# Four-layer sparse graph network: eager projection steps, whole first-layer rows, output by blocks

## The chip, the cores and the metric

The kernel runs on one core of one Trainium2 chip. The metric is the device time of the launch in microseconds, the median of several runs; lower is better. The engines named below are PE (matrix products and transposes), DVE (vector work), ACT (scalar engine), POOL (here it issues the indirect transfers) and SP (it issues the plain transfers).

## The reference

Sixteen graphs share one adjacency matrix of 1024 nodes, of which a fraction 0.0078 of the entries is set; each node of each graph has a row of 128 numbers. Four layers follow one another. Layers 0, 2 and 3 are attention blocks with 8 heads of 16, masked by the adjacency; layer 1 is a graph attention with one head.

```python
# layers 0, 2, 3
Q, K, V = h @ Wq, h @ Wk, h @ Wv                      # 8 heads of 16
scores = where(adj == 0, -inf, Q K^T / 4)             # per head
x = layer_norm(h + (softmax(scores) V) @ Wo + bo)
x = layer_norm(x + relu(x @ W1 + b1) @ W2 + b2)
# layer 1
h = x @ W;  e = leaky_relu(h a_src [i] + h a_dst [j]);  e = where(adj == 0, -inf, e)
x = layer_norm(softmax(e) h + x)
```

## The kernel before

The kernel works on the lists of neighbours and not on the full matrix. A setup of some 100 us reads the adjacency, sorts the nodes by degree and makes lists of neighbours. After it a tile `t` (8 of them) holds 128 nodes of similar degree, and `places` holds their row numbers in the input and the output. The graphs are split into two groups of 8 (`GR`), and each group again into two halves of 4 (`HF`, the index `h`).

A unit, or block, is one layer, one group and one tile; there are 4 x 2 x 8 = 64, numbered from 0 in that order, so that 0 to 7 are layer 0 with the first group, 8 to 15 layer 0 with the second, 48 to 63 the last layer. For a block the kernel gathers, by an indirect transfer on POOL (line 942), the keys and values of up to two neighbours of each node at a time, multiplies them with the queries on DVE (954), adds up the heads (977), takes exponentials on ACT (981), multiplies with the values on DVE (1005) and sums over the neighbours on PE with 0/1 matrices (1021). One such round is a piece; a block has 4 to 6 of them. At the end of a block `divided` divides by the sums (1058, 1061), and `attention_tail`, one generator for each half, does the rest of the layer (output projection, norms, feed-forward) while the next block's pieces run. Its last step is `finish`: in layers 0 to 2 it projects the result into the next layer's table of keys and values in DRAM, and in the last layer it transposes back into a tile `outs` and sends it by an indirect transfer on POOL to the rows of `out` (676), one transfer of 256 KB for each half.

Everything is issued in an order written out by hand: `manual_schedule`, with generators that are advanced a step at a time. Each engine executes its own instructions in that order. The main loop (line 1152) goes over the pieces and calls `others` three times for a piece of an attention layer. `others` advances the tails at a pace, and then one step of the first thing it finds among `fronts` (the next block's queries, slot lists and weights), `loads` (the input of the block after the next) and `slow`. `slow` is `at_leisure(1)` (772): the projection of the second group's rows into the keys and values of layer 0, 16 half-tiles of three steps each (transposes; two graphs' projection; the other two graphs', after which the table is written). It is advanced only while no tail is in its last stage, or while it is itself in the middle of a half-tile:

```python
def idle():
    return slow if held[0] or not busy[0] else []
```

The first group's rows are projected in the setup (`at_once`). Gathers run four pieces ahead. The first gather of block 8 needs the second group's whole table, so `gathered` (929) first drains what is left of `slow`.

`loaded` (840) fetches the input of a block. In layer 0 that is, for each half, an indirect transfer on POOL of 256 KB into a buffer `rows`, and, some steps later, four transposes on PE and a copy on ACT into the input buffer `x`. `x` has four buffers. The buffer of the second half has the tag of the query buffer `q`.

Of the kernel before, what the change touches and what calls it, by code (L numbers as in the profile page):

```python
# [14 lines left out]
F32 = mybir.dt.float32  # L15
# [7 lines left out]
P = 128  # L23
D = 128
# [113 lines left out]
def sparse_path(ctx: ExitStack, tc: tile.TileContext, a: dict, out: bass.AP, flag):  # L138
# [42 lines left out]
    idx = const.tile([P, 2, T, J, QUADS], I32, name="idx")  # L181
    marks = const.tile([P, len(MARK), 32], F32, name="marks")
    nc.gpsimd.memset(marks, 0.0)
    places = const.tile([P, GR, HF, T], I32, name="places")
    bad = const.tile([P, T], F32, name="bad")
    seen = const.tile([P, 2, G * H], F32, name="seen")
    nc.gpsimd.memset(seen, 0.0)
# [38 lines left out]
    def graph(wide):  # L226
# [148 lines left out]
                q = row_of(t, j)  # L375
                nc.vector.tensor_copy(there[rows, t : t + 1], node[rows, q : q + 1])
        for g in range(GR):
            for h in range(HF):
                nc.vector.tensor_scalar(
                    places[:, g, h, :], there, float(GR * HF), float(g * HF + h),  # L380
                    ALU.mult, ALU.add,
                )
        low = s1.tile([P, T], F32, name="low")
        nc.vector.tensor_tensor(bad, sorted_[:, :, 2], caps[:, :T], ALU.is_gt)
        nc.vector.tensor_scalar(low, sorted_[:, :, 2], 1.0, None, ALU.is_lt)
# [252 lines left out]
    def turned(z, dst, gain=None, shift=None, dve=False):  # L638

        ps = bank([P, GH, P])  # L640
        for i in range(GH):
            nc.tensor.transpose(ps[:, i, :], z[:, i, :], ident)  # L642
        if dve and gain is None:
            nc.vector.tensor_copy(dst, ps)
        elif dve:
            nc.vector.tensor_scalar(dst, ps, gain, shift, ALU.mult, ALU.add)
        elif gain is None:
            nc.scalar.copy(dst, ps)  # L648
        else:
            nc.scalar.activation(dst, ps, AF.Identity, bias=shift, scale=gain)  # L650

    def over_graphs(v):
        return v.rearrange("p (o d) -> p o d", o=1).to_broadcast([P, GH, D])

    def finish(l, g, t, h, z, gain, shift, dve=False):
        if l + 1 < len(LAYERS):

            wanted[0] = True
            while held[0]:
                advance(slow)  # L660
            wanted[0] = False
            busy[0] += 1
            xn = states.tile([P, GH, P], F32, tag="xT", name="xT")
            turned(z, xn, gain, shift)
            yield "free"
            yield from project(l + 1, g, t, h, xn)
            busy[0] -= 1
            return
        xn = states.tile([P, GH, P], F32, tag="xT", name="xT")
        turned(z, xn, gain, shift, dve)  # L670
        yield
        o = twos.tile([P, GH, D], F32, tag="kv", name="outs")
        turned(xn, o, dve=dve)
        yield
        yield
        nc.gpsimd.indirect_dma_start(  # L676
            out=out.rearrange("n (k c) -> (n k) c", k=GR * HF),
            out_offset=bass.IndirectOffsetOnAxis(ap=places[:, g, h, t : t + 1], axis=0),
            in_=o.rearrange("p g d -> p (g d)"), in_offset=None,
        )  # L680

    def hidden():
        return ones_.tile([P, F * GH * P], F32, tag="f1", name="f1")
# [74 lines left out]
    def natural(g, t, h, rows, kv=None):  # L758

        xn = states.tile([P, GH, P], F32, tag="xT", name="xT")  # L760
        turned(rows, xn)
        yield
        yield from project(0, g, t, h, xn, kv)
# [7 lines left out]

    def at_leisure(g):
        def fetch(k):
            rows = ones_.tile([P, GH, D], F32, tag="xg", name="xg")
            if k < T * HF:
                nc.sync.dma_start(
                    rows.rearrange("p g d -> p (g d)"),
                    a["x"][k // HF * P : (k // HF + 1) * P, columns(g, k % HF)],
                )
            return rows  # L780

        rows = fetch(0)
        yield
        for k in range(T * HF):
            steps = natural(g, k // HF, k % HF, rows)
            held[0] = True
            next(steps)
            rows = fetch(k + 1)
            yield
            yield from steps  # L790
            held[0] = False
            if wanted[0]:
                yield
# [46 lines left out]
    def loaded(u):  # L840

        if u >= len(units):
            return
        l, g, t = units[u]
        xs[units[u]] = inputs.tile([P, HF, GH, P], F32, tag="x", name="x")
        if l == 0:
            def fetch(h):
                if u == 0:
                    rows = twos.tile([P, GH, D], F32, tag="o", name="rows")
                else:  # L850
                    rows = ones_.tile([P, GH, D], F32, tag="q" if h else "rows", name="rows")
                nc.gpsimd.indirect_dma_start(
                    out=rows.rearrange("p g d -> p (g d)"), out_offset=None,
                    in_=a["x"].rearrange("n (k c) -> (n k) c", k=GR * HF),
                    in_offset=bass.IndirectOffsetOnAxis(ap=places[:, g, h, t : t + 1], axis=0),
                )
                return rows

            rows = fetch(0)
            yield "idle"  # L860
            yield "idle"
            yield
            turned(rows, xs[units[u]][:, 0])
            rows = fetch(1)
            yield "idle"
            yield "idle"
            yield
            turned(rows, xs[units[u]][:, 1])
            yield
            return  # L870
        nc.sync.dma_start(
            xs[units[u]].rearrange("p h g n -> p (h g n)"),
            kept[l, g][t].rearrange("p h c -> p (h c)"),
        )
# [220 lines left out]
    def others():  # L1095
        pace[0] += pace[1]
        while pace[0] >= 1.0:
            advance(tails)
            pace[0] -= 1.0
        while True:  # L1100
            gens = fronts or loads or idle()
            if not gens:
                break
            got = next(gens[0], "end")
            if got == "end":
                gens.pop(0)
                continue
            if got == "idle":
                advance(idle())
            break  # L1110

    with tc.manual_schedule():
        wide = [gather_buffer() for _ in range(EDGES)]
# [38 lines left out]
        for i in range(len(parts) + 2):  # L1152
            here = i < len(parts)
            u = parts[i][0] if here else len(units)
            if here:
                l = units[u][0]
                if i and parts[i - 1][0] != u:
                    begun = i
                    if u < T - 1:
                        fronts.append(islice(rest, 4))  # L1160
                    if l + 1 < len(LAYERS) and LAYERS[l + 1][1] is ATTN:
                        if units[u][1:] == (0, 1):
                            more = load_weights(LAYERS[l + 1][0])
                            next(more)
                            next(more)
                        if units[u][1:] == (0, 4):
                            fronts.append(more)
                if is_attention(u):
                    products(i)
            if i > 1:  # L1170
                summed(i - 2)
                done = parts[i - 2][0]
                if parts[i - 1 : i] == [] or parts[i - 1][0] != done:
                    closing = divided(done)
                    next(closing)
            others()
            if here:
                exponentials(i)
            if here and i == begun + 1:
                if is_attention(u):  # L1180
                    shared(u)
                while loads:
                    advance(loads)
                if u + 1 < len(units):
                    fronts.append(queries(u + 1))
                loads.append(loaded(u + 2))
                if u:
                    advance(loads)
            others()
            if 0 < i <= len(parts):  # L1190
                weighted(i - 1, 0)
                if not is_attention(parts[i - 1][0]):
                    others()
                    weighted(i - 1, 2)
                gathered(i - 1 + AHEAD)
                for _ in sizes:
                    pass
            if closing is not None and here:
                while any(gen not in free for gen in tails):
                    advance(tails)  # L1200
                next(closing)
                sizes, closing = closing, None
                passes = 3 if is_attention(u) else 4
                steps = STEPS if is_attention(done) else GRAPH_STEPS
                steps -= LATE[units[done][0]]
                pace[:] = 0.0, steps / (passes * sum(part[0] == u for part in parts) - 1)
            others()
            if i + 1 >= len(parts) or parts[i + 1][0] != u:

                while fronts:  # L1210
                    advance(fronts)
# [441 lines left out]
```

## Time and profile before

| | us |
|---|---|
| median of three runs | 2280.79 |
| lowest and highest | 2275.02, 2287.53 |
| span of the profiled execution | 2290.8 |
| PE, DVE, ACT, POOL busy in it | 2052.0, 1871.1, 1530.3, 1050.7 |

The page gives no time of the profiled execution beside its span. Times in the timelines are counted from the start of the span. The end of a block, where it is needed, is taken at the reciprocal on DVE (line 1058). Busy time of an engine says how full it is over the whole span; what a stage waits for is read from the timelines and waits of that stage. Blocks 2 to 6 take 40.6 to 42.1 us each, block 7 takes 46.0, block 8 takes 44.5, blocks 9 to 14 take 36.5 to 37.7, layer 1's blocks 12 to 25, and those of the last layer 36.3 to 41.4, but for the last, 28.4.

### The profile page before, as it was taken

The page shows a single profiled execution, that of the slowest core. Times are in us where ns is not written, and L with a number is a line of the kernel's source. Part 1 is how long each engine was busy: PE and PEld are TensorE (multiplying, and loading weights), DVE is VectorE, ACT ScalarE, POOL GpSimd, SP SyncE. Part 2 cuts the span into 40 slices and gives each one's busy share as a digit, 9 for nine tenths or more (in the row PEclk, how much of TensorE's full clock was granted, in tenths as well). Part 3 has the DMA queues.
Part 4 walks back from the last instruction along what each step waited for, and adds up shares of the span by engine and source line. Part 5 has one row for each costly group of instructions (what it writes and reads, how often), then busy time and mean ns, then how long its engine had stood idle before and what let it go on. Part 6 is the DMA issues. An engine that isn't in the chain of part 4 may idle for free. (4 is left out here: it accounts for less than half of the span.)

```text
span 2290.8 us, 36572 instructions
## 1 busy us (share of the span) xinstructions
PE 2052.0 (90%) x13140; PEld 1271.6 (56%) x13140; DVE 1871.1 (82%) x1472; ACT 1530.3 (67%) x5041; POOL 1050.7 (46%) x730
## 2 busy tenths in 40 slices
PE   6479999899998999998899989999999988998987
PEld 5336666555555555554465655655655555555544
DVE  7898888588888477777988889988888887988783
ACT  3237777777776565556677777777777766776765
POOL 3355344245445278884443434333344444444540
PEclk8789999999999999999999999999999998999999
DMA  7868888678887699997998978888887877677750
GB/s 249 278 217 300 304 279 305 240 247 302 285 295 265 197 330 354 354 373 288 326 318 292 319 254 306 296 314 295 281 282 277 291 258 250 242 275 270 260 217 20
DMA packets 165197, 636.06 MB, mean 278 GB/s; under 512 B 35064, under 2 KB 37880, under 8 KB 116510
## 3 DMA queue, kind: packets, MB, share of 16 engines
q0 software_dynamic: 89216, 485.08, 59.3%
q1 hardware_dynamic: 75792, 148.57, 18.9%
q8 instruction: 105, 1.72, 0.3%
q14 instruction: 84, 0.69, 0.1%
HBM read 581.08 MB, written 92.34 MB: 294 GB/s over the span
## 5 line engine op out<-in xcount | busy, mean ns | idle before, releaser
L942 POOL DMA_INDIRECT e<-table,idx x576 | 844.2, 1466 | 1022.1 <-DVE pr L1005 796.6
L1005 DVE TENSOR_TENSOR pr<-e,ex 128x2048 f32<-128x2048 f32 (+1 forms) x320 | 661.3, 2075 | 55.9 <-ACT ex L981 32.7
L954 DVE TENSOR_TENSOR pr<-e,qr 128x2048 f32<-128x2048 f32 x192 | 439.7, 2290 | 160.3 <-DMA e<-table,idx 91.5
L1021 PE MATMUL acc<-pr,marks 128*32 128x512 f32 x2624 | 528.5, 616 | 20.3 <-DVE pr L1005 16.4
L977 DVE TENSOR_REDUCE sc<-pr 128x128 f32<-128x2048 f32 (+1 forms) x240 | 497.5, 2073 | 8.0
L620 ACT ACTIVATE z<-yps,root 128x128 f32<-128x128 f32 x888 | 319.0, 390 | 35.6 <-PE yps L735 16.8
L1021 PEld LDWEIGHTS acc<-pr,marks 128*32 128x32 f32 x2624 | 108.7, 111 | 280.9 <-issue 231.6
L635 ACT ACTIVATE z<-yps,rstd 128x128 f32<-128x128 f32 x888 | 255.0, 371 | 7.2
L731 PE MATMUL yps<-W,f 128*128 128x128 f32 x1520 | 252.6, 283 | 7.7 <-ACT f L726 1.9
L726 ACT ACTIVATE f<-ps,b 128x512 f32<-128x512 f32 x190 | 130.6, 695 | 160.4 <-PE ps L717 159.7
L731 PEld LDWEIGHTS yps<-W,f 128*128 128x128 f32 x1520 | 205.7, 193 | 51.7 <-issue 26.2
L572 PE MATMUL ps<-Wkv,xT 128*128 128x256 f32 x768 | 212.2, 417 | 20.0 <-ACT xT L648 14.4
L908 ACT COPY qr<-ps 128x512 f32<-128x512 f32 x384 | 197.1, 602 | 47.7 <-PE ps L905 47.7
L642 PE MATMUL ps<-ident,z 128*128 128x128 f32 x896 | 179.7, 300 | 41.4 <-ACT z L635 36.6
L642 PEld LDWEIGHTS ps<-ident,z 128*128 128x128 f32 x896 | 116.2, 143 | 167.7 <-ACT z L635 86.5
L717 PE MATMUL ps<-x,W 128*128 128x512 f32 x384 | 193.9, 630 | 12.5 <-ACT x L650 12.4
L620 ACT ACTIVATION_READ_ACCUMULATOR z<-yps,root 128x1 f32 x888 | 203.7, 229 | 0.0
L905 PE MATMUL ps<-q,rep 32*128 32x512 f32 x768 | 166.5, 661 | 36.4 <-ACT q L900 34.0
L572 PEld LDWEIGHTS ps<-Wkv,xT 128*128 128x128 f32 x768 | 146.5, 204 | 73.9 <-ACT qr L908 18.0
L981 ACT ACTIVATE ex<-sc 128x128 f32<-128x128 f32 (+1 forms) x240 | 76.4, 318 | 157.9 <-DVE sc L977 157.8
L576 ACT COPY kv<-ps 128x512 f32<-128x512 f32 x176 | 103.3, 593 | 108.1 <-PE ps L572 85.8
L706 PE MATMUL yps<-Wo,oT 128*128 128x128 f32 x768 | 159.9, 291 | 10.0 <-ACT oT L648 10.0
(174 smaller groups left out, 2724.2 us busy)
## 6 DMA issues: line engine op xcount, KB each, us to landing
table<-kv SPq DMA_DIRECT2D x88, 512.0 KB
kept<-xT SPq DMA_DIRECT2D x96, 256.0 KB
x<-kept SPq DMA_DIRECT2D x48, 512.0 KB
qx<-qr SPq DMA_DIRECT2D x48, 256.0 KB
e<-table,idx POOLq DMA_INDIRECT x576
table<-kv SPq DMA_DIRECT2D x32, 256.0 KB
qx<-qr SPq DMA_DIRECT2D x18, 384.0 KB
qx<-qr SPq DMA_DIRECT2D x42, 128.0 KB
```

Of the source, the lines that this page charges most:

```text
L572: nc.tensor.matmul(ps[:, k, :], x[:, i + k, :], w[LAYERS[l][0], "Wkv"], start=True, stop=True,)
L620: nc.scalar.activation(z[:, i, :], y[:, i, :], AF.Square, scale=D**-0.5, bias=root, accum_out=total[:, i : i + 1],)
L635: nc.scalar.activation(z[:, i, :], y[:, i, :], AF.Copy, scale=rstd[:, i : i + 1])
L642: nc.tensor.transpose(ps[:, i, :], z[:, i, :], ident)
L717: nc.tensor.matmul(ps, p["W1"][:, f * P : (f + 1) * P], x1.rearrange("p g n -> p (g n)"), start=True, stop=True,)
L731: nc.tensor.matmul(ps[:, i, :], f1[:, f, i * P : (i + 1) * P], p["W2"][:, f, :], start=(f == 0), stop=False,)
L908: nc.scalar.copy(qs[u][:, j, h * GH * D : (h + 1) * GH * D], pss[j])
L942: nc.gpsimd.indirect_dma_start(out=es[i][:, k, :], out_offset=None, in_=tables[l, g][:, :], in_offset=bass.IndirectOffsetOnAxis(ap=idx[:, ...
L954: nc.vector.tensor_tensor(prs[i][0][:, :n, :], es[i][:, :n, :ROW], qx[u].rearrange("p (o c) -> p o c", o=1) if (MIX, 0) in piece else of_p ...
L977: nc.vector.tensor_reduce(sc[:, :n, :], prs[i][0][:, :n, :].rearrange("p k (a d) -> p k a d", d=HD), mybir.AxisListType.X, ALU.add,)
L1005: nc.vector.tensor_tensor(prs[i][k0 // 2][:, :m, :].rearrange("p k (a d) -> p k a d", d=d), es[i][:, k0 : k0 + m, base : base + ROW].rearr ...
L1021: nc.tensor.matmul(outs[32 * j : 32 * j + 32], marks[:, mark, :], rhss, start=(chunk == mine[0]), stop=(chunk == mine[-1]),)
```

## The change

- `places` holds one row number for each node and group, and no longer one for each half; `halves` holds those of the very last block, for each half.
- Output: both halves of a block are written into one tile `outs` of 512 KB, and one indirect transfer sends it when the second half is done. The very last block keeps a transfer for each half.
- The rows of the second group in `at_leisure` have two buffers, `xg` and `xh`, and are fetched two half-tiles ahead.
- `loaded` fetches a block's layer-0 rows with one indirect transfer of 512 KB straight into the input buffer `x`; each half is transposed on PE and copied back by ACT into the same place.
- `others` ends with one more step of `idle()`, that is of `slow`, while the current block is 0 or 1.

```diff
     def finish(l, g, t, h, z, gain, shift, dve=False):
...
-        o = twos.tile([P, GH, D], F32, tag="kv", name="outs")
-        turned(xn, o, dve=dve)
-        yield
-        yield
-        nc.gpsimd.indirect_dma_start(
-            out=out.rearrange("n (k c) -> (n k) c", k=GR * HF),
-            out_offset=bass.IndirectOffsetOnAxis(ap=places[:, g, h, t : t + 1], axis=0),
-            in_=o.rearrange("p g d -> p (g d)"), in_offset=None,
-        )
+        if h == 0:
+            leaving[g, t] = twos.tile([P, HF, GH, D], F32, tag="kv", name="outs")
+        o = leaving[g, t]
+        turned(xn, o[:, h], dve=dve)
+        yield
+        yield
+        if (l, g, t) == units[-1]:
+            nc.gpsimd.indirect_dma_start(
+                out=out.rearrange("n (k c) -> (n k) c", k=GR * HF),
+                out_offset=bass.IndirectOffsetOnAxis(ap=halves[:, h : h + 1], axis=0),
+                in_=o[:, h].rearrange("p g d -> p (g d)"), in_offset=None,
+            )
+        elif h + 1 == HF:
+            nc.gpsimd.indirect_dma_start(
+                out=out.rearrange("n (k c) -> (n k) c", k=GR),
+                out_offset=bass.IndirectOffsetOnAxis(ap=places[:, g, t : t + 1], axis=0),
+                in_=o.rearrange("p h g d -> p (h g d)"), in_offset=None,
+            )
...
     def at_leisure(g):
         def fetch(k):
-            rows = ones_.tile([P, GH, D], F32, tag="xg", name="xg")
+            rows = ones_.tile([P, GH, D], F32, tag=("xg", "xh")[k % 2], name="xg")
...
-        rows = fetch(0)
+        ahead = [fetch(0), fetch(1)]
         yield
         for k in range(T * HF):
-            steps = natural(g, k // HF, k % HF, rows)
+            steps = natural(g, k // HF, k % HF, ahead.pop(0))
             held[0] = True
             next(steps)
-            rows = fetch(k + 1)
+            ahead.append(fetch(k + 2))
...
     def loaded(u):
...
-            def fetch(h):
-                if u == 0:
-                    rows = twos.tile([P, GH, D], F32, tag="o", name="rows")
-                else:
-                    rows = ones_.tile([P, GH, D], F32, tag="q" if h else "rows", name="rows")
-                nc.gpsimd.indirect_dma_start(
-                    out=rows.rearrange("p g d -> p (g d)"), out_offset=None,
-                    in_=a["x"].rearrange("n (k c) -> (n k) c", k=GR * HF),
-                    in_offset=bass.IndirectOffsetOnAxis(ap=places[:, g, h, t : t + 1], axis=0),
-                )
-                return rows
-
-            rows = fetch(0)
-            yield "idle"
-            yield "idle"
-            yield
-            turned(rows, xs[units[u]][:, 0])
-            rows = fetch(1)
-            yield "idle"
-            yield "idle"
-            yield
-            turned(rows, xs[units[u]][:, 1])
+            x = xs[units[u]]
+            nc.gpsimd.indirect_dma_start(
+                out=x.rearrange("p h g d -> p (h g d)"), out_offset=None,
+                in_=a["x"].rearrange("n (k c) -> (n k) c", k=GR),
+                in_offset=bass.IndirectOffsetOnAxis(ap=places[:, g, t : t + 1], axis=0),
+            )
+            for h in range(HF):
+                yield "idle"
+                yield "idle"
+                yield
+                turned(x[:, h], x[:, h])
             yield
             return
...
             if got == "idle":
                 advance(idle())
             break
+        for _ in range(eager[0]):
+            advance(idle())
+
+    eager = [1]
...
                 l = units[u][0]
+                eager[0] = 1 if u < 2 else 0
```

More of the change, by code (lines that the diff above doesn't have):

```diff
@@ L183, in sparse_path @@
     nc.gpsimd.memset(marks, 0.0)
-    places = const.tile([P, GR, HF, T], I32, name="places")
+    places = const.tile([P, GR, T], I32, name="places")
+    halves = const.tile([P, HF], I32, name="halves")
     bad = const.tile([P, T], F32, name="bad")
@@ L377, in graph @@
         for g in range(GR):
[L378 to L381, printed above, removed]
-                )
+            nc.vector.tensor_scalar(
+                places[:, g, :], there, float(GR), float(g), ALU.mult, ALU.add,
+            )
+        for h in range(HF):
+            nc.vector.tensor_scalar(
+                halves[:, h : h + 1], there[:, T - 1 :], float(GR * HF), float((GR - 1) * HF + h),
+                ALU.mult, ALU.add,
+            )
         low = s1.tile([P, T], F32, name="low")
@@ L653, in over_graphs @@
         return v.rearrange("p (o d) -> p o d", o=1).to_broadcast([P, GH, D])
+    leaving = {}
     def finish(l, g, t, h, z, gain, shift, dve=False):
@@ L671, in finish @@
         yield
-        o = twos.tile([P, GH, D], F32, tag="kv", name="outs")
-        turned(xn, o, dve=dve)
+        if h == 0:
+            leaving[g, t] = twos.tile([P, HF, GH, D], F32, tag="kv", name="outs")
+        o = leaving[g, t]
+        turned(xn, o[:, h], dve=dve)
         yield
         yield
-        nc.gpsimd.indirect_dma_start(
-            out=out.rearrange("n (k c) -> (n k) c", k=GR * HF),
-            out_offset=bass.IndirectOffsetOnAxis(ap=places[:, g, h, t : t + 1], axis=0),
-            in_=o.rearrange("p g d -> p (g d)"), in_offset=None,
-        )
+        if (l, g, t) == units[-1]:
[9 more added lines that the diff above has]
+                in_=o.rearrange("p h g d -> p (h g d)"), in_offset=None,
+            )
     def hidden():
@@ L846, in loaded @@
         if l == 0:
-            def fetch(h):
-                if u == 0:
-                    rows = twos.tile([P, GH, D], F32, tag="o", name="rows")
-                else:
-                    rows = ones_.tile([P, GH, D], F32, tag="q" if h else "rows", name="rows")
-                nc.gpsimd.indirect_dma_start(
-                    out=rows.rearrange("p g d -> p (g d)"), out_offset=None,
-                    in_=a["x"].rearrange("n (k c) -> (n k) c", k=GR * HF),
-                    in_offset=bass.IndirectOffsetOnAxis(ap=places[:, g, h, t : t + 1], axis=0),
-                )
-                return rows
-            rows = fetch(0)
-            yield "idle"
-            yield "idle"
-            yield
-            turned(rows, xs[units[u]][:, 0])
-            rows = fetch(1)
-            yield "idle"
-            yield "idle"
-            yield
-            turned(rows, xs[units[u]][:, 1])
+            x = xs[units[u]]
[3 more added lines that the diff above has]
+                in_offset=bass.IndirectOffsetOnAxis(ap=places[:, g, t : t + 1], axis=0),
+            )
+            for h in range(HF):
+                yield "idle"
+                yield "idle"
+                yield
+                turned(x[:, h], x[:, h])
             yield
```

## The prediction

> **What bounds the kernel now.** I read the page first, then the stage table by blocks (a block is one unit: layer, group, tile; its end is the reciprocal of line 1058), then the waits of each engine, and at the two stalls the timelines.
>
> The first part of the page:
>
> ```profile
> PE 2052.0 (90%) x13140; PEld 1271.6 (56%) x13140; DVE 1871.1 (82%) x1472; ACT 1530.3 (67%) x5041; POOL 1050.7 (46%) x730
> ```
>
> PE and DVE share the load, so each stage has to be asked. The stage table (length, PE, PEld, DVE, ACT, POOL, clock, DMA share, GB/s): blocks 0 and 1; block 4; block 7; block 10; a layer-2 block; a last-layer block.
>
> ```profile
> 101.00:162.50 61.50, 34.17 (x151) 14.06 (x151) 57.66 (x77) 10.98 (x25) 29.34 (x17) 0.72 0.68 249
> 162.50:203.20 40.70, 37.80 (x252) 24.79 (x252) 35.81 (x39) 30.63 (x99) 17.80 (x12) 1.00 0.77 274
> 328.50:370.00 41.50, 38.74 (x258) 25.63 (x258) 35.51 (x38) 31.07 (x102) 18.15 (x12) 1.00 0.83 291
> 410.60:456.70 46.10, 39.94 (x246) 27.22 (x247) 25.78 (x16) 30.79 (x98) 15.65 (x12) 0.93 0.64 229
> 575.30:612.70 37.40, 34.72 (x237) 22.10 (x235) 32.21 (x18) 28.21 (x98) 18.31 (x12) 1.00 0.85 296
> 1438.10:1474.70 36.60, 34.39 (x229) 21.66 (x229) 32.24 (x20) 27.60 (x88) 14.18 (x10) 1.00 0.91 321
> 2110.50:2148.50 38.00, 33.17 (x216) 20.02 (x216) 32.12 (x20) 27.04 (x87) 18.10 (x12) 1.00 0.72 264
> ```
>
> Block 0 leaves PE idle for 27 us. Blocks 2 to 6 take some 41.5 us and blocks 9 to 14 some 37: the former also carry the second group's projection (two half-tiles each). Block 7 is the longest, though it has the fewest pieces. The last layer has less PE work than layer 2 and is slower.
>
> Block 7 on SP, POOL and DVE (start, length):
>
> ```profile
> 416.72 0.57 SPq L581 DMA_DIRECT2D table<-kv  x1
> 422.34 4.04 SPq L581 DMA_DIRECT2D table<-kv  x2
> 429.70 0.99 POOL L942 DMA_INDIRECT e<-table,idx  x1 [27.85 <-DMA table<-kv]
> 432.00 2.29 DVE L1005 TENSOR_TENSOR pr<-e,ex 128x2048 f32<-128x2048 f32 x1 [10.37 <-ACT ex L981]
> ```
>
> The drain of line 930 emits the last three half-tiles at once; the first gather of the second group waits 27.85 us for their tables, and the exponential that DVE needs stands behind their copies on ACT.
>
> A last-layer block, on ACT, POOL and DVE:
>
> ```profile
> 2072.84 0.59 ACT L648 COPY outs<-ps 128x512 f32<-128x512 f32 x1 [0.27 <-PE ps L642]
> 2075.65 2.11 POOL L676 DMA_INDIRECT out<-outs,places  x1 [0.30 <-ACT qr L908]
> 2084.50 2.32 POOL L676 DMA_INDIRECT out<-outs,places  x1 [6.74 <-ACT rstd L627]
> 2087.12 1.95 POOL L942 DMA_INDIRECT e<-table,idx  x1 [0.31 <-ACT z L620]
> 2097.07 2.29 DVE L954 TENSOR_TENSOR pr<-e,qr 128x2048 f32<-128x2048 f32 x1 [5.46 <-DMA e<-table,idx]
> ```
>
> And DVE's waits from 1696 to 2224 us (total, times, longest):
>
> ```profile
> DVE pr L954 <- DMA e<-table,idx: 62.8, 14, 5.9
> ```
>
> The second half's data are ready at 2073.4, yet its output goes at 2084.50, and the gathers behind it on POOL go later still. The releaser printed had nothing to do with it. What did, the chain that ended last shows, at the very end where nothing else runs:
>
> ```profile
> 2282.70 0.99 DMA out<-outs,places
> 2283.69 2.30 issue
> ```
>
> Output h=1 follows output h=0 only when that has landed: both write the tensor `out` at rows taken from a table, so the second is ordered behind the first. In the stream that costs POOL some 6 us of waiting and DVE 4.5 us (62.8 / 14) in each of blocks 49 to 62.
>
> **The Trainium skill.** "DMA: Bandwidth & Descriptors", section "Anatomy of one DMA — SWDGE (gpsimd) path": a semaphore wait is made on the issuing sequencer before dispatch, so it holds what is behind; the trace agrees (2075.65 to 2087.12 without a gather). It prices a DMA at 2.0 us plus bytes / 436e3: an estimate of 2.6 us for 256 KB; the trace has 3.5 us (2282.70 to 2286.19) alone and 8.4 to 8.9 among gathers, which I use. Same page, "Issuing engines are not separate DMA queues": SP's and POOL's transfers share the same engines, so early projections compete with gathers; blocks 0 and 1 will show it. "TensorE: Matmul & The Clock Gate", section "What's actually happening": a little-used PE runs throttled; block 0 shows a clock of 0.72, so extra work there also raises it.
>
> **The change, part by part.**
>
> *Extra steps.* A half-tile of `at_leisure` is three steps; from block 4's timeline PE pays 0.60 (four transposes) + 1.89 (projection) = 2.49 us, ACT three copies of 0.59, DMA 256 KB in and 512 KB out, 0.79 MB. `others` runs three times a piece: 18 times in block 0 (6 pieces), 15 in block 1 (5). No tail is in its last stage there, so `idle()` isn't empty and all 33 extra steps act. With some 8 steps of their own these blocks reach step 41; step 1 fetches, half-tile k is written at step 5 + 3k: 0 to 12 are written, where now it is 0 to 2 (146, 182, 197 us). Ten move: one out of block 3, two each out of 4, 5 and 6, three out of block 7.
> Block 4 to 6: PE 38.7 - 5.0 = 33.7, below DVE's 35.5 (slot lists included); with the bubbles of now, 38.0 instead of 41.6: 3 x 3.6 = 10.8, and 1.8 in block 3. Block 7: 46.1 to 33.5 (block 15, the same tile, takes 32.6): 12.5. Block 8 refills for 44.5 us; 40 and 48, the same tile, take 41.4, so 3.1, say 3.5 with what it no longer inherits. Sum 28.6.
> Cost: 10 x 2.49 = 24.9 us of PE in 102.2 us with 72.0 busy: at block 4's 93%, 103.9 us if spread evenly (+1.7); but block 1 alone, with 4.5 more half-tiles, needs (37.8 + 11.2) / 0.933 = 52.5 instead of 40.7 (+11.8). DMA: 26.5 MB moved there now, 34.4 then: 116 us at block 10's 296 GB/s (+14), 99 at the 346 GB/s reached from 176 to 197 us (0). I take +10, between 0 and +20. A step's transposes wait on PE for their rows; behind them stand the accumulating matmuls of line 1021, for whose release of `pr` DVE waits, with four buffers in between. Fetching two ahead removes the rest of that wait (4.8 us in two places now): counted at nothing; without it those 4.8.
> Net -18.6.
>
> *Output.* One DMA of 512 KB a block, at the place of the second, waits only for the output a block earlier, 37 us before, and for copies done at 2073.4. The 6 us on POOL go, and the 2.1 us of the other DMA. What is late next is PE: 33.2 us busy at full clock, which at 95%, what stages full of PE work reach (34.39 of 36.60 above, 35.48 of 37.00 in block 48), is 35.0 us; DVE needs 32.1. Average now (2224.46 - 1696.02) / 14 = 37.75. So 14 x 2.75 = 38.5; at least 0, at most 62.8. The buffer is held from h=0 until landed; two buffers, next needed two blocks later, so no new wait. The last block keeps two DMAs and the same end.
>
> *First-layer rows.* 16 POOL DMAs of about 1 us plus 0.3 go; POOL is mostly waiting for DVE there, so they are hidden. PE's waits for `rows` (9.1 us, partly in the setup) shrink, and the second half's rows no longer share a buffer with `q`. The rows now need `x` free at fetch: of four buffers the oldest is two blocks old and last read by line 707, a block earlier. The copy in place waits for the same transposes as before. I take -1, between +2 and -5. The index columns (four DVE operations as before) cost nothing; the two row buffers cover each other's space.
>
> *Sum.* -18.6 - 38.5 - 1 = -58.1: the profiled span goes from 2290.8 to 2232.7. The page gives no other time of that execution; its span is 10 us above the median, so I subtract from the median: 2280.8 - 58.1 = 2222.7, 2223.
>
> **Rivals.** (a) The output stall stays, since POOL waits for something else or PE fills the gap: only -19.6, 2261. For it: PE is 33 of 38 us busy. Against: layer 2, with more PE work, runs at 36.6. (b) The first layer nets nothing: the steps find `idle()` empty, or cost in blocks 0 and 1 what they save: 2280.8 - 39.5 = 2241. For it: block 1's PE is 93% busy. (c) Neither acts: 2281. (d) Slower: the early transfers starve the gathers. It decides when blocks 0 and 1 fall below 34.4 MB / (102.2 + 28.6 + 38.5 + 1 + 11.4) = 189 GB/s; at 180 they last 191 us, +89, and the time is 2302. Against: apart from the tail, no 57 us slice of the page falls below 197.
>
> **How the numbers follow.** Forecast 0.62, (a) 0.14, (b) 0.13, (c) 0.05, (d) 0.06. 0.5% is 11.4 us, about what a measurement here can tell. (a) lies near that bound, so I move 0.02 of it: faster 0.87, same 0.07, slower 0.06. The range runs from -85 (output -60, first layer -24) to just past (a): 2196 to 2262, leaving out (c), (d) and a little.
>
> **What would show it.** Right: `xg`/`xh` fetches end before 300 us; no 27.85 us wait for `table<-kv`; blocks 4 to 6 near 38 us, block 7 near 33; in the last layer 17 output DMAs, no POOL gap before them, DVE's wait for `e` far below 62.8, blocks near 35. Wrong: blocks 0 and 1 together over 122 us; last-layer blocks still near 37.7, with DVE's idle time now put down to PE.

## The result and the profile after

The changed kernel takes 2252.68 us (median of 6 runs, 2241.01 to 2259.04) against 2280.56 for the kernel before in the same series (2275.02 to 2287.53); the ratio is 0.9861, 95% interval 0.9838 to 0.9884. That is 28 us between the medians, 32 by the ratio; where a gain in us stands beside a ratio below, it is worked out from the ratio. The forecast was 2223 us, within 2196 to 2262: the direction and the range held, the gain is about half of the 58 us forecast. The profiled span went from 2290.8 to 2251.9 us.

The first part of the page after. PE is still the fullest engine, and nearly as busy as before in absolute time: the change took away waits, and hardly any work.

```profile
PE 2043.1 (91%) x13140; PEld 1271.3 (56%) x13140; DVE 1872.9 (83%) x1472; ACT 1528.3 (68%) x5041; POOL 1016.3 (45%) x699
```

The stage table after, for the stages shown before: blocks 0, 1, 4, 7 and 10, a layer-2 block and a last-layer block (length, PE, PEld, DVE, ACT, POOL, clock, DMA share, GB/s).

```profile
101.00:161.80 60.80, 47.58 (x233) 28.72 (x234) 55.49 (x76) 22.91 (x47) 22.84 (x15) 0.88 0.92 331
161.80:213.70 51.90, 48.15 (x303) 33.67 (x302) 35.76 (x40) 36.54 (x111) 15.87 (x11) 0.97 0.80 282
294.40:332.10 37.70, 35.71 (x239) 22.53 (x242) 35.75 (x39) 28.31 (x98) 17.74 (x11) 1.00 0.80 276
406.30:440.00 33.70, 30.82 (x209) 20.31 (x210) 25.87 (x15) 25.43 (x88) 14.22 (x10) 0.95 0.76 265
521.10:557.60 36.50, 33.83 (x236) 21.37 (x235) 32.20 (x18) 28.16 (x98) 15.76 (x12) 1.00 0.86 307
1414.80:1450.90 36.10, 33.67 (x229) 21.58 (x229) 32.20 (x19) 27.75 (x89) 14.36 (x10) 1.00 0.94 325
2079.50:2115.30 35.80, 32.57 (x213) 19.62 (x212) 32.35 (x19) 26.30 (x86) 17.09 (x11) 1.00 0.78 280
```

Block 0 now holds 47.6 us of PE work instead of 34.2, at the same length and a higher clock (0.88 for 0.72). Block 1 pays: 51.9 us for 40.7. Block 4 is down from 41.5 to 37.7, block 7 from 46.1 to 33.7. The last-layer block is down from 38.0 to 35.8, but DVE still needs only 32.4 of it.

Where the time went is read from the ends of the blocks (the reciprocal of `divided`), before minus after, added up:

| up to the end of block | gained, us |
|---|---|
| 1 | -10.4 |
| 3 | -7.9 |
| 7 | 16.7 |
| 8 | 16.8 |
| 13 | 18.6 |
| 15 | 24.6 |
| 48 | 21.5 |
| 62 | 38.2 |

The first layer gives some 18 us, the last one 16.7 (blocks 49 to 62: 36.55 us each instead of 37.75). The 6 us between 13 and 15 can't be put down to an edit: block 15 takes 27.8 to 32.8 us over the kernels below, and the changed kernel itself takes 27.8 us there in this profile and 30.7 in a second one.

The two stalls that the prediction showed, after. On SP, the table writes that stood in block 7: the 14th half-tile of the second group is written at 207.72, in block 1, and the last two in block 2.

```profile
207.72 0.52 SPq L585 DMA_DIRECT2D table<-kv  x1
233.91 16.15 SPq L585 DMA_DIRECT2D table<-kv  x2
```

No gather waits for `table<-kv` any more. On POOL, in a last-layer block, one output, and no wait before it or behind it but for a buffer that DVE frees:

```profile
1713.07 0.99 POOL L946 DMA_INDIRECT e<-table,idx  x1 [0.30 <-issue]
1714.36 2.09 POOL L691 DMA_INDIRECT out<-outs,places  x1 [0.30 <-ACT qr L912]
1720.35 1.76 POOL L946 DMA_INDIRECT e<-table,idx  x1 [3.90 <-DVE pr L1009]
1722.41 1.00 POOL L946 DMA_INDIRECT e<-table,idx  x1 [0.30 <-issue]
```

And yet DVE still waits for a gather some 15 us later, where the 4.5 us were before (DVE; then DVE's waits from 1674.6 to 2186.3 us: total, times, longest):

```profile
1735.12 2.29 DVE L958 TENSOR_TENSOR pr<-e,qr 128x2048 f32<-128x2048 f32 x1 [4.47 <-DMA e<-table,idx]
```

```profile
DVE pr L958 <- DMA e<-table,idx: 29.3, 10, 4.7
DVE pr L958 <- PE acc L1025: 11.9, 7, 3.4
DVE pr L1009 <- ACT ex L985: 4.8, 3, 3.9
```

The wait for gathers went from 62.8 to 29.3 us (34.9 in a second profile of the changed kernel); part of the rest became other waits of DVE. What holds them is the question of the second set of experiments.

### The profile page after: what moved, and what is told of

Read it like the earlier page. It is cut to its first block, busy times and chain, and to the rows that moved or that the text cites. A ratio compares the mean times of both kernels' runs of the same rounds, so it can differ in the third digit from the quotient of the medians.

```text
span 2251.9 us, 36507 instructions
## 1 busy us (share of the span) xinstructions
PE 2043.1 (91%) x13140; PEld 1271.3 (56%) x13140; DVE 1872.9 (83%) x1472; ACT 1528.3 (68%) x5041; POOL 1016.3 (45%) x699
## 4 chain that ended last, share of the span: by engine, by line
PE 41%; ACT 18%; issue 16%; DVE 11%; DMA 9%; POOL 5%; POOLq 0%; DVEq 0%; ACTq 0%
PE acc L1025 9%; DMA e<-table,idx 8%; PE yps L746 5%; PE ps L576 4%; POOL e L946 4%; PE ps L646 4%; ACT qr L912 4%; PE ps L732 3%; PE ps L909 3%; DVE pr L958 3%; ACT z L624 3%; DVE sc L981 3%; DVE pr L1009 2%; PE yps L750 2%; ACT z L639 2%
## 5 line engine op out<-in xcount | busy, mean ns | idle before, releaser
L946 POOL DMA_INDIRECT e<-table,idx x576 | 854.1, 1483 | 1101.8 <-DVE pr L1009 902.1
L1025 PE MATMUL acc<-pr,marks 128*32 128x512 f32 x2624 | 519.1, 608 | 14.8 <-DVE pr L1009 10.8
L576 PE MATMUL ps<-Wkv,xT 128*128 128x256 f32 x768 | 215.0, 419 | 20.0 <-ACT xT L652 16.7
L909 PE MATMUL ps<-q,rep 32*128 32x512 f32 x768 | 175.3, 661 | 34.7 <-ACT q L904 33.5
L732 PE MATMUL ps<-x,W 128*128 128x512 f32 x384 | 190.4, 620 | 12.5 <-ACT x L654 12.5
L722 PE MATMUL yps<-centre,x 128*128 128x128 f32 x768 | 155.5, 285 | 3.6
```

The costliest lines, as they stand in the source:

```text
L576: nc.tensor.matmul(ps[:, k, :], x[:, i + k, :], w[LAYERS[l][0], "Wkv"], start=True, stop=True,)
L732: nc.tensor.matmul(ps, p["W1"][:, f * P : (f + 1) * P], x1.rearrange("p g n -> p (g n)"), start=True, stop=True,)
L946: nc.gpsimd.indirect_dma_start(out=es[i][:, k, :], out_offset=None, in_=tables[l, g][:, :], in_offset=bass.IndirectOffsetOnAxis(ap=idx[:, ...
L1025: nc.tensor.matmul(outs[32 * j : 32 * j + 32], marks[:, mark, :], rhss, start=(chunk == mine[0]), stop=(chunk == mine[-1]),)
```

## The experiments: the parts

Theory after the result: the steps give the first layer's gain and the output the last layer's, the rows nothing, and the parts add up. The rival: they depend on one another. All four ran on one chip, with a kernel before of 2283.29 us.

**Steps alone.** The kernel before with

```diff
             if got == "idle":
                 advance(idle())
             break
+        for _ in range(eager[0]):
+            advance(idle())
...
+                eager[0] = 1 if u < 2 else 0
```

> The kernel before with the extra projection steps in blocks 0 and 1 alone (one row buffer, fetched one half-tile ahead). Theory: the first layer's gain is the steps' own; the changed kernel's trace stands 16.8 us earlier at the end of block 8 and 18.6 us at block 13, so some -18 us: 2262, with block 1 near 52 us instead of 40.7 and block 7 near 34 instead of 46. The last layer stays as before, near 37.7 us a block. Rival: without the second row buffer each extra step's transposes wait on PE for their rows, and blocks 0 and 1 cost 5 us or more beyond that: 2267 or more.

Measured: 2280.24 us, ratio 0.9981 (0.9969 to 0.9992): 4 us, not 18. Blocks 3 to 7 are as short as in the changed kernel (block 7: 33.7), but block 0 ends at 173.6 instead of 161.8 and block 1 takes 58.9 us instead of 51.9. On PE (start, length) and then, for the tile `xg`, what PE waited for:

```profile
118.92 1.99 PE L572 MATMUL ps<-Wkv,xT 128*128 128x256 f32 x8 [0.73 <-ACT xT L648]
127.75 1.09 PE L642 MATMUL ps<-ident,xg 128*128 128x128 f32 x4 [6.84 <-DMA xg<-in_x]
129.57 2.08 PE L572 MATMUL ps<-Wkv,xT 128*128 128x256 f32 x4 [0.73 <-ACT xT L648]
131.58 3.62 PE L1021 MATMUL acc<-pr,marks 128*32 128x512 f32 x16
```

```profile
  DMA xg<-in_x: 16.4, 5
```

The eager transposes reach PE before their rows have landed (arrived in the buffer; 4.3 us after their issue in the median), and the sums of line 1021 stand behind them. The rival of this run is right: the steps are worth little without the second buffer, and the 19 us by which block 1 ends later than in the changed kernel are of the size of these waits. (They are no exact measure: in the profiles of kernels without these steps block 0 ends between 160.4 and 168.7.)

**Output alone.** The kernel before, with the new end of `finish` (one tile for both halves, one transfer a block).

> The kernel before with the output sent by blocks alone. Theory: the last layer gains 1.2 us a block over 14 blocks as in the changed kernel's trace, -17 us: 2264; the first layer's blocks are as before (block 7 near 46). Rival: the last layer's gain comes in part from the other edits, or the prediction's 2.75 us a block is right and something else took it back: below -8 or above -30 us.

Measured: 2271.90 us, ratio 0.9927 (0.9900 to 0.9953), 17 us. Blocks 49 to 62 take 36.51 us each, as in the changed kernel; the first layer is not shortened (block 7: 45.4). The last layer's gain is the output's, and all of it.

**Rows alone.** The kernel before, with the new `loaded`.

> The kernel before with the first-layer rows fetched whole into the input buffer alone. Theory: -1 us, hidden, within 4 us of before. Rival: the 5 us that the changed kernel gains at the end of the first layer (block 15: 27.8 instead of 32.6) come from here, because PE no longer waits for rows: -5 to -8 us.

Measured: 2284.76 us, ratio 0.9999 (0.9984 to 1.0014): nothing. Block 15 takes 29.4 us here, but 29.3 in the run with the output alone, too, and 32.8 in a later kernel that has these rows: it is not theirs.

**Without the steps.** The changed kernel with

```diff
-                eager[0] = 1 if u < 2 else 0
+                eager[0] = 0
```

> The changed kernel without the extra steps. Theory: parts add up, so it stands 18 us above the changed kernel, near 2263 to 2270 where before is 2281. Rival: the parts overlap (an earlier block 7 gives the later edits room or takes it), and it differs from output_only by more than 6 us.

Measured: 2266.19 us, ratio 0.9905 (0.9885 to 0.9926). The steps are then worth 0.0044, some 10 us (3 to 17, if the two intervals are taken together), in the changed kernel and 4 alone. Whether the second buffer also helps the drain that comes back here (block 7: 43.2 us for 46.0) can't be told: the interval overlaps that of the output alone.

**One row buffer.** The changed kernel with

```diff
-            rows = ones_.tile([P, GH, D], F32, tag=("xg", "xh")[k % 2], name="xg")
+            rows = ones_.tile([P, GH, D], F32, tag="xg", name="xg")
...
-        ahead = [fetch(0), fetch(1)]
+        ahead = [fetch(0)]
...
-            ahead.append(fetch(k + 2))
+            ahead.append(fetch(k + 1))
```

> The changed kernel with one buffer for the second group's rows, fetched one half-tile ahead, as before. Theory: the second buffer is what makes the extra steps cheap; without it PE waits some 16 us for rows in blocks 0 and 1, which end near 230 us instead of 213.7, and the kernel stands 12 to 18 us above the changed one. Rival (the prediction's): at most 5 us.

Measured, on the chip of the changed kernel run again: ratio 0.9934 (0.9911 to 0.9957) against 0.9858 (0.9822 to 0.9894). The buffer is worth 0.0076, 17 us (8 to 27, the two intervals taken together); block 1 ends at 235.8, where it ends at 212.8 with two on this chip. What PE waited for with one buffer, and then with two in the changed kernel:

```profile
  DMA xg<-in_x: 15.6, 5
```

```profile
  DMA xg<-in_x: 0.2, 1
```

This is the clearest answer on the first layer: the steps and the buffer are one edit. The steps alone give 4 us, and the buffer without the steps can't be told from nothing.

**The changed kernel again**, as the yardstick of that chip.

> The changed kernel itself, on the chip of the three others, as their yardstick: 0.986 of the kernel before, between 0.984 and 0.989.

Measured: 2257.77 us, ratio 0.9858 (0.9822 to 0.9894), as expected.

**Steps in block 0 alone**, one and then two at each place:

```diff
-                eager[0] = 1 if u < 2 else 0
+                eager[0] = 1 if u < 1 else 0
```

> The changed kernel with the extra steps in block 0 alone. Theory (PE's idle time in block 0 is free, block 1 pays in full): block 1 falls from 51.9 us back to about 45, blocks 3 to 5 rise by 2 to 4 us each to 41.5, the drain in block 7 stays empty: within 4 us of the changed kernel either way. Rival (the cost of block 1 is the transfers' and not PE's): it gains 6 us or more.

> The changed kernel with two extra steps at each place, in block 0 alone: 36 steps there. Theory: some 12 half-tiles need 30 us of PE where 27 are idle at a low clock, and 9.4 MB of transfers beside the first gathers, so block 0 grows by 5 to 15 us and block 1 falls by 7: between -6 and +8 us against the changed kernel. Rival: the idle time takes them all and it is 8 us or more faster.

Measured: one step, ratio 0.9842 (0.9806 to 0.9877), the same as the changed kernel's within the noise: block 1 takes 43.5 us instead of 51.9, blocks 3 to 5 take 41.6, 42.1 and 41.0 again, and block 7 stays at 32.7. Two steps, 0.9891 (0.9858 to 0.9924): block 0 ends at 180.1 instead of 161.8, more than the 5 to 15 us expected. There an instruction that DVE needs for the weights of the tails stands behind the projections on PE (DVE's waits from 95 to 162 us):

```profile
DVE b L522 <- PE ps L517: 12.0, 1, 12.0
```

So block 0 takes some six half-tiles for nothing and no twelve, and what those in block 1 cost there is saved again in blocks 3 to 5. No version beat the changed kernel clear of its interval.

## The experiments: the last layer

**The second output to another tensor.** The kernel before with

```diff
+    aside = dram.tile([N, B * D], F32, name="aside")
...
+        elsewhere = h and (l, g, t) != units[-1]
         nc.gpsimd.indirect_dma_start(
-            out=out.rearrange("n (k c) -> (n k) c", k=GR * HF),
+            out=(aside if elsewhere else out).rearrange("n (k c) -> (n k) c", k=GR * HF),
```

> The kernel before, with the output of each second half sent to another tensor in DRAM, but for the last block's (so half of the output is left out of the result); the number, size and place of the transfers stay. Theory: the second output waited for the first one's landing because both write one tensor; without that order the wait of some 6 us on POOL before it goes, and the last layer's blocks 49 to 62 take about what sending by blocks gave, 36.5 us instead of 37.7: 2264. Rival: POOL waits for something else (room for descriptors, the copies): gaps of 6 us stay, 37.7 us a block, 2281.

Measured: ratio 0.9955 (0.9939 to 0.9971); blocks 49 to 62 take 36.66 us. Both outputs are there, and the gap between them is gone (POOL):

```profile
1778.40 2.11 POOL L678 DMA_INDIRECT out<-outs,places  x1 [0.30 <-ACT qr L910]
1780.81 0.98 POOL L678 DMA_INDIRECT aside<-outs,places  x1 [0.30 <-issue]
```

So it was the order of two writes to one tensor, and neither the number of transfers nor their size, that cost these 1.1 us a block (1.2 with the output by blocks; two profiles of the changed kernel differ by 0.2). As a whole this kernel gains 10 us where the output by blocks gains 17; its block 48 already ends 5 us later than before, for which the edit gives no reason, and that difference stays open.

**What is late next** was PE in the prediction. Two kernels take half of one candidate away: the bytes of the gathers, or a part of PE's work; the third takes the output away.

```diff
-            width = 2 * ROW if names is ATTN else ROW + G
+            width = (ROW if l == 3 else 2 * ROW) if names is ATTN else ROW + G
...
-        base, d = (ROW, HD) if is_attention(u) else (0, D)
+        base, d = (0 if units[u][0] == 3 else ROW, HD) if is_attention(u) else (0, D)
```

(`project` then writes the keys alone.)

> The changed kernel with a last-layer table of keys alone: its gathers fetch 512 KB a neighbour column instead of 1 MB, and the keys stand in for the values (the last layer's result is not the reference's); DVE, PE and ACT do the same work. Theory A (landing of the gathers, crowded after the short shared piece, sets the idle time of DVE): blocks 49 to 62 fall from 36.55 to below 35, -20 us or more. Theory B (PE's lag sets it): they stay above 35.8.

```diff
-        for f in range(F):
+        fs = 1 if l == 3 and not last else F
+        for f in range(fs):
             ps = bank([P, GH * P])
...
-            for f in range(F):
+            for f in range(fs):
                 nc.tensor.matmul(
```

> The changed kernel with half of the feed-forward's width left out in the last layer, but for the last block (its result is not the reference's): PE does some 4 us less a block, ACT 1.4, the gathers are the same. Theory B (PE's lag): blocks 49 to 62 fall from 36.55 to 34 or 35, -20 us or more. Theory A (landing): they stay above 35.8.

```diff
-        elif h + 1 == HF:
+        elif h + 1 == HF and t == T - 1:
             nc.gpsimd.indirect_dma_start(
```

> The changed kernel with the output sent only for the last tile of each group (7 of 8 tiles' outputs are left out). Theory: once it waits for nothing, the output costs little more than its 0.5 MB of traffic; blocks 49 to 62 stay within 0.6 us of the changed kernel's 36.55. Rival: the single 512 KB transfer still holds POOL for 2.1 us or delays the gathers' landing, and it is what keeps DVE idle 3.6 us a block: near 34 us a block, -30 us in all.

Measured, blocks 49 to 62 (us each), beside the ratio of the whole kernel:

| kernel | block | ratio to the kernel before |
|---|---|---|
| before | 37.75 | |
| changed, two profiles | 36.55, 36.34 | 0.9861 (0.9838 to 0.9884) |
| few outputs | 35.99 | 0.9808 (0.9741 to 0.9875) |
| less work on PE | 36.34 | 0.9800 (0.9741 to 0.9858) |
| half the gathers | 34.44 | 0.9683 (0.9624 to 0.9742) |

The stage table over those blocks, for the kernel before, the changed one, the one with half the gathers and the one with less PE work:

```profile
1696.00:2224.50 528.50, 475.74 (x3012) 287.06 (x3012) 450.19 (x253) 373.76 (x1209) 245.02 (x167) 0.95 0.74 266
```

```profile
1674.60:2186.30 511.70, 471.43 (x3012) 288.11 (x3011) 452.93 (x253) 372.99 (x1209) 234.74 (x153) 0.96 0.79 274
```

```profile
1670.00:2152.10 482.10, 459.12 (x3008) 280.98 (x3007) 452.66 (x252) 372.05 (x1209) 256.93 (x153) 0.98 0.55 168
```

```profile
1680.00:2188.80 508.80, 434.41 (x2729) 252.85 (x2728) 453.04 (x252) 355.50 (x1181) 236.48 (x153) 0.93 0.78 276
```

DVE's work is the same in all four; length less DVE's busy time is 78, 59, 29 and 56 us. Taking 37 us of PE's work away (2.6 us a block, where 4 were expected) brings 3 us, or nothing against the second profile of the changed kernel; taking half of the gathers' bytes away brings 30. Theory A stands: in the changed kernel the landing of the gathers is late next. In the kernel with half of them PE is 95% busy, the share at which the prediction put PE's bound; no run asked whether PE is what holds that kernel. DVE's waits for gathers in that kernel, and in the one with less PE work:

```profile
DVE pr L959 <- DMA e<-table,idx: 8.0, 8, 1.6
```

```profile
DVE pr L959 <- DMA e<-table,idx: 44.2, 13, 5.3
```

Why they land late at a mean of 274 GB/s, below the 299 of layer 2 (blocks 33 to 46), is only read from the timeline: around a short piece (its first product takes 1.22 us on DVE, and not 2.29) DVE frees three buffers within some 12 us (1717.80, 1722.39 and 1729.44 are the multiplications that do it), and POOL issues six gathers of 1 MB between 1720 and 1734 us. These six take 11.7 us to land in the median, 12.9 at most, where all of blocks 49 to 62 take 9.3. No run here spread them out, and in those layer-2 blocks the median is 9.9, where DVE waits 19.2 us for gathers and not 29.3, so the burst isn't shown to be the reason. The run without most outputs moves the block by 0.35 to 0.56 us, as the theory had it: the output itself is not what is left.

## Why the prediction was right or wrong

- **Extra steps.** The count was good: 13 half-tiles by the end of block 1 were forecast and 14 came. The run without the steps writes 3 there, so they brought 11 of three steps each: all 33 acted. Blocks 4 to 6 saved 12.2 us (forecast 10.8), block 3 2.5 (1.8), block 7 12.3 (12.5), and blocks 0 and 1 cost 10.4 (10). Block 1 took 51.9 us where the sum of PE's work gave 52.5. Only block 8 was mis-sized: 0.2 us saved and 3.5 forecast. It takes 44.3 to 44.5 us in every kernel, also where nothing is left to drain, so its length is no refill after the drain. Net 16.8 at block 8, 18.6 forecast.
- **Second row buffer.** The step "counted at nothing; without it those 4.8" failed in the second half. Undone, it costs 17 us (0.9934 for 0.9858). The 4.8 us were taken from a schedule in which a half-tile was written every 15 to 36 us in blocks 0 to 6; in the changed kernel one is written every 4 to 14 us in blocks 0 and 1, and at such a pace a fetch one half-tile ahead is waited for (15.6 us). A wait has to be priced at the pace of the changed kernel.
- **Output, the wait.** Right: the printed releaser (ACT) was false, the chain of the last 4 us had the true one, and another tensor removed the gap.
- **Output, the size.** The failed step is "What is late next is PE", with 35.0 us a block and 38.5 us in all. It is the gathers' landing, at 36.55 us and 16.8 us in all. The prediction put all of DVE's 62.8 us of waits for gathers down to the output's stall; 29.3 of them remain without it. Its table had DMA at 0.72 in that stage and 0.91 in layer 2, and a mean share doesn't say whether a gather lands in time. Rival (a), with PE filling the gap, was wrong too: the gain is half, not none.
- **Output, two readings.** The 35.0 was low even as a PE bound: it takes one block's 33.2 us, where the mean over the 14 blocks is 33.7 in the changed kernel (471.43 / 14), 35.4 at the same 95%. And the 35.48 of 37.00 that the prediction calls block 48 is block 49 (1696.0 to 1733.0). No output is sent in that block (the first goes at 1735.9), so it had no stall to lose, and it takes 36.9 us after the change; block 48 has PE busy for 37.84 of 41.40 us.
- **Layer 2 as a measure.** Its 36.8 us a block (blocks 33 to 46 of the kernel before) are close to what the last layer now takes, but not by the same wait: PE is busy for 94% of that time, and DVE waits 33.0 us for PE and 13.0 for gathers. The likeness is not shown to be more than chance.
- **Rows.** Forecast -1, measured 0.9999. Hidden, as argued.
- **Sum.** By blocks 18.6 + 16.7 = 35 us, with the rest of the span's 39 from block 15 and layers 1 and 2, which vary between kernels; by the timed ratio 32. The rivals with neither gain and with starved gathers did not come: blocks 0 and 1 moved 308 GB/s together (331 and 282), where the slower rival needed them below 189.
- **The Trainium skill.** "DMA: Bandwidth & Descriptors", section "Anatomy of one DMA — SWDGE (gpsimd) path", on the wait at the issuing sequencer, agrees with the run to another tensor: the gathers behind it came free. "TensorE: Matmul & The Clock Gate", section "What's actually happening", agrees in block 0: more PE work at the same length, clock 0.88 for 0.72.

## What to carry to other kernels

When a releaser named by the profile was done long before, look for an order that the tensors impose, such as two scatters into one output; the end of the kernel, where nothing else runs, shows it plainly. When a stall is removed, the busiest engine's work is only one bound on what remains: price the transfers' landing beside it, and take half of each candidate away in a run to see which one holds, as was done here. Work that is moved earlier comes at another pace, so its fetches have to be deepened with it, and priced at the new pace.

## What was not expected of the hardware

A half-tile's rows (256 KB) land in 4.3 us in the median with one buffer (the steps alone) and in 7.8 us with two (6.5 in the second profile); PE's waits for them fall all the same from 16.4 to 0.2 us. That more is in flight at a time with two would explain the longer landing, but no run separates it from the other traffic.
